# Keys and values of the 64-wide heads by seven block products instead of eight, with the order of the matrix engine written out

## The chip, the cores and the metric

The kernel runs on one core of one Trainium2 chip. A core has a matrix engine (TensorE, PE in the profile), a vector engine (VectorE, DVE), an activation engine (ScalarE, ACT), a general engine (GpSimd, POOL) and a queue engine (SyncE, SP) that mostly issues transfers. Each engine works through its own queue in order and waits on semaphores for the others. Matrix products are written to PSUM, an accumulator memory of eight banks; the other operands lie in SBUF. All data is float32. The metric is the device time of one execution in microseconds (us).

## What is computed

A decoder of two layers on x (8 batches, 256 tokens, 256 features). Layer 0 is self-attention with heads of 16, cross-attention over the context and an expert stage; layer 1 is self-attention, a cross-attention with 16 heads of 64 and an added null key and value, and a stage of 8 experts with a shared expert. The change lies in the cross-attention with heads of 64, cut here to what matters:

```python
x = x + _L1_xattn_ref(_layernorm(x, axis=-1), ctx_2048, Wq, Wkv, null_kv, Wout, ln_scale, ln_bias)
# inside, HEADS, DH = 16, 64; context is (8, 256, 512), Wkv is (512, 2048)
q = _split_heads(jnp.einsum('bnd,df->bnf', x, Wq))
kv = jnp.einsum('bmc,cf->bmf', context, Wkv)
k, v = jnp.split(kv, 2, axis=-1)
k, v = (_split_heads(k), _split_heads(v))
k = jnp.concatenate((nk, k), axis=-2)      # the null key and value
v = jnp.concatenate((nv, v), axis=-2)
sim = jnp.einsum('bhid,bhjd->bhij', q * DH ** -0.5, k)
out = jnp.einsum('bhij,bhjd->bhid', jax.nn.softmax(sim, axis=-1), v)
out = jnp.einsum('bnf,fd->bnd', out.transpose(0, 2, 1, 3).reshape(b, -1, 1024), Wout)
out = (out - mu) * jax.lax.rsqrt(var + EPS) * ln_scale + ln_bias
```

For each batch the keys and values are one product of a 256x512 context with a 512x2048 weight.

## The kernel before

`plain` (line 156) holds the whole decoder; `null_cross_attention` (line 1043) is the stage that is changed. A part that is a loop over the eight batches b follows a first part for b = 0 alone.

**The pieces of one batch.** `keys` (L1058) loads the transposed context `ctxT` and makes kT (features by tokens) by `features` (L1047): four PSUM tiles `fm`, each of two feature blocks of 128, each block four matrix products over the 512 inputs. `vals` (L1065) makes v (tokens by features) in four tiles `vps` of 512 features. `queries` (L1082) makes the null logits `nps` and then qT in four tiles `fm`. `weighted` (L1092) runs the attention: per pair of heads c it forms scores `stx` (L1100), their exponentials `pTx` on ACT (L1104), the sum `both` of the two token halves on POOL (L1106), the column sums `den` on PE (L1114, `sums`) and the weighted values `ox` on PE (L1138). `reciprocals` (L1152) turns `den` into 1/sum on DVE (L1155, L1156) and sends it through DRAM (`rd`, `rs`, L1160 and L1162) to spread it over partitions; `divide` (L1184) multiplies it into oT, half on DVE and half on POOL. `outward` (L1190) is the output projection `wo`, copied to `yx` on ACT, normalised on DVE and POOL (L256 on POOL is the power -1/2 of the variance) and added to x by six POOL instructions (L1203 to L1205). `routed_norm`, `routed_rows` and `routed_scores` (L953 to L966) prepare the previous batch for the expert stage.

**The order.** One batch in the loop is `weighted(b)`, then transposes for batch b+1 and b-1, `reciprocals(b)`, `keys(b+1)`, `routed_scores(b-1)`, `vals(b+1)`, `divide(b)`, `outward(b)`, `queries(b+1)`. Instructions are given to a scheduler that settles each engine's queue when the program is built; where `manual_schedule` names an engine, that engine's order is the order of the text. Here that holds for PE in the last batch and after it. The scheduler also puts in the semaphore waits: an instruction that writes a tile waits for those that read it.

**Product and tiles.** Every 128-wide product goes through one helper as two matmuls of 64 output rows, and each float32 matmul shows as two records in the trace:

```python
def product(out, lhsT, rhs, start, stop):
    for h in (slice(0, 64), slice(64, P)):
        nc.tensor.matmul(out[h], lhsT[:, h], rhs, start=start, stop=stop, skip_group_check=True)
```

All of them carry the helper's line L274, so they are told apart by their tiles. PSUM is shared by three pools (L564 to L566): `mm` with three one-bank tiles (fm, vps, nps, wo, ox and the transposes), `scp` with two tiles of two banks (stx, and hx of the shared expert), `op` with one (den). In SBUF the exponentials take a ring of four buffers with the tag "pT". `load_shared` (L920) loads the shared expert's weights ws13 and ws2 early, before the loop.

Of the kernel before, what the change touches and what calls it, by code (L numbers as in the profile page):

```python
# [28 lines left out]
F32 = mybir.dt.float32  # L29
# [4 lines left out]
ALU = mybir.AluOpType  # L34
# [4 lines left out]
P = 128  # L39
B, S, D = 8, 256, 256  # L40
# [115 lines left out]
def plain(  # L156
# [747 lines left out]
    def ended(t):  # L904

        nc.gpsimd.memset(t[tail:, full, :], 0.0)
        return t
# [9 lines left out]
    norms = [(const.tile([P, 2, 2], F32, name=f"mean{b}"), const.tile([P, 2], F32, name=f"rstd{b}")) for b in range(B)]  # L917
    shared = {}

    def load_shared():  # L920

        router = pool_s.tile([P, 2, E], F32, name="router")
        nc.gpsimd.dma_start(router, a["L1_ffn_router_DE"].rearrange("(c p) e -> p c e", p=P))
        xnT = pool_s.tile([P, 2, B * S], F32, name="xnTe")
        ws13 = w_in(pool_s, a["L1_ffn_ws1_DF"], a["L1_ffn_ws3_DF"], "ws13")
        ws2 = w_out(ended(pool_s.tile([P, NFC, D], F32, name="ws2")), a["L1_ffn_ws2_FD"])
        shared.update(router=router, xnT=xnT, ws13=ws13, ws2=ws2)

    def hidden(mid, first, n, pair, silu):

# [109 lines left out]

    def null_cross_attention(phase):
        work = phase.enter_context(tc.tile_pool(name="d2", bufs=2))
        scale = XD**-0.5

        def features(dst, w, rows, copy):  # L1047
            n = w.shape[1]
            for c2 in range(0, nc8, 2):
                ps = mm.tile([P, 2, S], F32, tag="mm", name="fm")  # L1050
                for i in range(2):
                    for cc in range(n):
                        product(
                            ps[:, i, :], w[:, cc, (c2 + i) * P : (c2 + i + 1) * P], rows[:, cc, :], cc == 0, cc == n - 1
                        )
                copy(dst[:, c2 : c2 + 2, :], ps)

        def keys(b):  # L1058
            ctxT = ctxs.tile([P, CTX // P, S], F32, tag="ctxT", name="ctxT")
            nc.sync.dma_start(ctxT, a["ctx_T"][b].rearrange("(c p) t -> p c t", p=P))  # L1060
            kT = work.tile([P, nc8, S], F32, tag="kT", name="kTx", bufs=1)
            features(kT, wkv_x, ctxT, nc.scalar.copy)
            return ctxT, kT

        def vals(ctxT):  # L1065
            v = work.tile([P, 2, XH, XD], F32, tag="vx", name="vx", bufs=1)
# [13 lines left out]
            return v  # L1080

        def queries(xnT):  # L1082
            nps = mm.tile([P, 2, S], F32, tag="mm", name="nps")
            for k in range(2):
                product(nps[:, 0, :], wn[:, k].rearrange("p g w -> p (g w)"), xnT[:, k, :], k == 0, k == 1)
            qT = work.tile([P, nc8, S], F32, tag="qT", name="qTx", bufs=1)
            features(qT, wq_x, xnT, nc.vector.tensor_copy)
            en = work.tile([P, S], F32, tag="en", name="en")
            nc.scalar.activation(en, nps[:, 0, :], AF.Exp, scale=scale)
            return qT, en  # L1090

        def weighted(kT, v, qT):  # L1092


            def exp_scores(c):
                st = scp.tile([P, 2, 2, S], F32, tag="sc", name="stx")
                for kt in range(2):
                    for g in range(2):
                        rows = slice(XD * g, XD * (g + 1))
                        nc.tensor.matmul(  # L1100
                            st[:, g, kt, :], kT[rows, c, bass.ts(kt, P)], qT[rows, c, :], start=True, stop=True
                        )
                pT = work.tile([P, 2, 2, S], F32, tag="pT", name="pTx", bufs=4)
                nc.scalar.activation(pT, st, AF.Exp, scale=scale)  # L1104
                both = work.tile([P, 2, S], F32, tag="both", name="both", bufs=4)
                nc.gpsimd.tensor_tensor(both, pT[:, :, 0, :], pT[:, :, 1, :], ALU.add)  # L1106
                return pT, both

            oT = work.tile([P, nc8, S], F32, tag="oT", name="oT", bufs=1)
            den = op.tile([P, S], F32, tag="o", name="den")  # L1110

            def sums(c, both):
                for g in range(2):
                    nc.tensor.matmul(  # L1114
                        den[XD * g : XD * (g + 1), :],
                        hot8[:, c, :],
                        both[:, g, :],
                        start=c == 0,
                        stop=c == nc8 - 1,
                        skip_group_check=True,  # L1120
                    )

            def block(c2):
                return [exp_scores(c2 + i) for i in range(2)]


            ahead, before = block(0), []
            for c2 in range(0, nc8, 2):
                now = ahead
                if c2 + 2 < nc8:  # L1130
                    ahead = block(c2 + 2)
                for i, both in enumerate(before):
                    sums(c2 - 2 + i, both)
                o = mm.tile([P, 2, S], F32, tag="mm", name="ox")
                for i, (pT, _) in enumerate(now):
                    for kt in range(2):
                        for g in range(2):
                            nc.tensor.matmul(  # L1138
                                o[XD * g : XD * (g + 1), i, :],
                                v[:, kt, 2 * (c2 + i) + g, :],  # L1140
                                pT[:, g, kt, :],
                                start=kt == 0,
                                stop=kt == 1,
                                skip_group_check=True,
                            )
                (nc.vector.tensor_copy if c2 % 4 else nc.scalar.copy)(oT[:, c2 : c2 + 2, :], o)
                before = [both for _, both in now]
            for i, both in enumerate(before):
                sums(nc8 - 2 + i, both)
            return oT, den  # L1150

        def reciprocals(b, den, en):  # L1152

            r = work.tile([P, S], F32, tag="rx", name="rx")
            nc.vector.tensor_tensor(r, den, en, ALU.add)  # L1155
            nc.vector.reciprocal(r, r)  # L1156
            rd = dram.tile([2, nc8, S], F32, name=f"rd{b}")
# [6 lines left out]
                    rd[g : g + 1].rearrange("g c q -> g (c q)").to_broadcast([XD, nc8 * S]),  # L1164
                )
            nc.gpsimd.tensor_tensor(en, en, r, ALU.mult)
            low = work.tile([P, S], F32, tag="low", name="low")
            nc.vector.tensor_scalar(low, r, 1.0e-25, None, ALU.is_ge)
            nc.vector.scalar_tensor_tensor(
                low, r, 1.0e25, low, ALU.is_le, ALU.mult, accum_out=fit[:, b : b + 1]  # L1170
# [3 lines left out]
        def in_range():  # L1174

            for k in range(3):
                v = dens[:, k].rearrange("p t h -> p (t h)")
                low = work.tile([P, S], F32, tag="low", name="lowk")
                nc.vector.tensor_scalar(low, v, 1.0e-25, None, ALU.is_ge)
                nc.vector.scalar_tensor_tensor(  # L1180
                    low, v, 1.0e25, low, ALU.is_le, ALU.mult, accum_out=fit[:, B + k : B + k + 1]
                )
# [5 lines left out]
                )  # L1188

        def outward(b, oT, en):  # L1190
            y = work.tile([P, 2, D], F32, tag="y", name="yx")
            ps = mm.tile([P, 2, D], F32, tag="mm", name="wo")
            for t in range(2):
                cols = bass.ts(t, P)
# [21 lines left out]


        _, xnT = layernorm_T(0, work, mm)
        ctxT, kT = keys(0)
        v = vals(ctxT)  # L1220
        qT, en = queries(xnT)
        load_shared()
        order = ExitStack()
        for b in range(B):
            more = b + 1 < B
            oT, den = weighted(kT, v, qT)
            if more:
                _, xnT = layernorm_T(b + 1, work, mm)
            else:

                wproj.close()
                late = ctx.enter_context(tc.tile_pool(name="mids", bufs=1, side="right"))

                shared["mid_s"] = [ended(late.tile([P, NFC, 2 * S], F32, name=f"mid{i}")) for i in range(2)]
                routing_tables(late)
                order.enter_context(tc.manual_schedule(engines={mybir.EngineType.PE}))
            if b:
                routed_rows(b - 1, routed_norm(b - 1, work), work)
            rs, old = reciprocals(b, den, en), en
            if b == 1:  # L1240
                in_range()
            if more:
                ctxT, kT = keys(b + 1)
            if more:
                if b:
                    routed_scores(b - 1)
                v = vals(ctxT)
            else:
                for i, _ in enumerate(quarter(0)):
                    if i == 0:  # L1250
                        routed_scores(b - 1)
            divide(oT, rs)
            outward(b, oT, old)
            if more:
                qT, en = queries(xnT)
        order.close()
        with tc.manual_schedule(engines={mybir.EngineType.PE, mybir.EngineType.DVE}):
            for i, _ in enumerate(quarter(1)):
                if i == 1:
# [1227 lines left out]
```

## Time and profile before

Three runs took 1396.82, 1397.8 and 1399.36 us, a median of 1397.8. The execution that was profiled took 1396.5 us, with a span of 1394.8 us between its first and last instruction.

| stretch of the span, us | what runs | length, us | PE busy, us | DVE | ACT | POOL |
|---|---|---|---|---|---|---|
| 0 to 622.00 | layer 0 and self-attention of layer 1 | 622.00 | 596.49 | 309.07 | 274.47 | 184.88 |
| 622.00 to 658.85 | heads of 64: keys, values, queries of b = 0 | 36.85 | 36.75 | 3.89 | 5.67 | 0.86 |
| 658.85 to 721.58 | loop, b = 0 | 62.73 | 62.47 | 11.07 | 15.18 | 19.28 |
| 721.58 to 785.27 | loop, b = 1 | 63.69 | 63.37 | 16.41 | 15.66 | 21.52 |
| 785.27 to 1103.73 | loop, b = 2 to 6 | 318.46 | 316.86 | 71.88 | 78.32 | 104.26 |
| 1103.73 to 1150.85 | loop, b = 7 | 47.12 | 46.80 | 14.15 | 14.37 | 16.92 |
| 1150.85 to 1394.80 | experts | 243.95 | 234.81 | 75.91 | 53.69 | 47.94 |

A batch starts where its first score matmul `stx` starts. PE's clock is granted at 1.00 in every stretch of the loop. Matmuls overlap: a record's duration is its latency, and what a stream of them costs is the distance between starts.

### The profile page before, as it was taken

The page shows a single profiled execution, that of the slowest core. Times are in us where ns is not written, and L with a number is a line of the kernel's source. Part 1 is how long each engine was busy: PE and PEld are TensorE (multiplying, and loading weights), DVE is VectorE, ACT ScalarE, POOL GpSimd, SP SyncE. Part 2 cuts the span into 40 slices and gives each one's busy share as a digit, 9 for nine tenths or more (in the row PEclk, how much of TensorE's full clock was granted, in tenths as well). Part 3 has the DMA queues.
Part 4 walks back from the last instruction along what each step waited for, and adds up shares of the span by engine and source line. Part 5 has one row for each costly group of instructions (what it writes and reads, how often), then busy time and mean ns, then how long its engine had stood idle before and what let it go on. Part 6 is the DMA issues. An engine that isn't in the chain of part 4 may idle for free.

```text
span 1394.8 us, 28640 instructions
## 1 busy us (share of the span) xinstructions
PE 1357.5 (97%) x12198; PEld 884.4 (63%) x12198; DVE 502.4 (36%) x1467; ACT 457.4 (33%) x730; POOL 395.7 (28%) x499
## 2 busy tenths in 40 slices
PE   6999999999999999989999999999999999999998
PEld 3666756756766666665655656565656555688884
DVE  5443563563565654330222213131312225422213
ACT  2555444444444434431222313131322222122221
POOL 4222142052033234220332415152423412400004
PEclk9999999999999999999999999999999999999999
DMA  8960000000000006010101010110101010779954
GB/s 312 345 205 16 9 24 9 8 24 1 1 9 2 2 9 221 1 53 26 32 16 31 16 47 2 46 32 16 32 1 32 1 31 5 283 289 414 402 209 127
DMA packets 46921, 116.56 MB, mean 84 GB/s; under 512 B 8273, under 2 KB 30401, under 8 KB 42433
## 3 DMA queue, kind: packets, MB, share of 16 engines
q1 hardware_dynamic: 38912, 92.74, 19.3%
q0 software_dynamic: 5152, 18.89, 3.6%
q10 hardware_dynamic: 2720, 3.02, 0.6%
q8 instruction: 98, 1.61, 0.5%
q14 instruction: 39, 0.31, 0.1%
HBM read 104.00 MB, written 27.93 MB: 95 GB/s over the span
## 4 chain that ended last, share of the span: by engine, by line
PE 85%; DVE 5%; POOL 4%; issue 1%; ACT 1%; DMA 0%; ACTq 0%; POOLq 0%; DVEq 0%; SPq 0%
PE fm L274 12%; PE st L332 9%; PE o L364 9%; PE vps L274 8%; PE h L274 6%; PE wo L274 4%; PE ox L1138 4%; PE stx L1100 4%; PE out L1475 3%; PE out L1292 3%; PE h L947 3%; PE qk L274 3%; PE hx L947 3%; PE tr L281 3%; PE den L1114 2%; PE ao L274 2%
## 5 line engine op out<-in xcount | busy, mean ns | idle before, releaser
L364 PE MATMUL o<-pT,padv 128*64 128x256 f32 (+1 forms) x1536 | 171.6, 365 | 1.1 <-POOL pT L344 1.1
L341 ACT ACTIVATE pT<-st 128x1024 f32<-128x1024 f32 (+1 forms) x128 | 110.5, 915 | 88.8 <-PE st L332 87.9
L364 PEld LDWEIGHTS o<-pT,padv 128*64 128x64 f32 x1536 | 103.1, 137 | 52.7 <-issue 10.0
L332 PE MATMUL st<-qm,kT 64*128 64x256 f32 (+1 forms) x1024 | 117.2, 367 | 0.9 <-DVE qm L310 0.6
L274 PE MATMUL fm<-ctxT,wkv_x 128*64 128x256 f32 x1024 | 112.9, 380 | 0.0
L274 PE MATMUL vps<-wkv_x,ctxT 128*64 128x512 f32 x512 | 111.8, 593 | 0.0
L332 PEld LDWEIGHTS st<-qm,kT 64*128 64x128 f32 x1024 | 90.1, 189 | 26.0 <-issue 15.6
L274 PEld LDWEIGHTS fm<-ctxT,wkv_x 128*64 128x64 f32 x1024 | 73.0, 137 | 37.3 <-issue 1.3
L1106 POOL TENSOR_TENSOR both<-pTx 128x512 f32<-128x512 f32 x64 | 79.6, 1273 | 57.4 <-ACT pTx L1104 33.8
L1104 ACT ACTIVATE pTx<-stx 128x1024 f32<-128x1024 f32 x64 | 62.1, 1021 | 89.9 <-PE stx L1100 86.8
L274 PE MATMUL h<-xrT,w 128*64 128x128 f32 (+1 forms) x1936 | 86.9, 250 | 1.4 <-issue 1.4
L274 PEld LDWEIGHTS h<-xrT,w 128*64 128x64 f32 x1936 | 84.3, 137 | 4.4 <-issue 2.1
L274 PEld LDWEIGHTS vps<-wkv_x,ctxT 128*64 128x64 f32 x512 | 36.4, 137 | 68.9 <-issue 68.6
L341 ACT ACTIVATE pT<-st,kbias 128x1024 f32<-128x1024 f32 x64 | 68.0, 1113 | 28.7 <-PE st L332 28.7
L256 POOL TENSOR_TENSOR lnrs<-lnve,mhalf 128x2 f32<-128x2 f32 x48 | 34.2, 717 | 147.0 <-DVE lnve L254 95.2
L332 PE MATMUL st<-qm,memk 64*128 64x256 f32 x512 | 68.8, 393 | 0.5
L939 ACT ACTIVATE sl<-h 128x128 f32<-128x128 f32 (+1 forms) x114 | 35.4, 310 | 96.1 <-PE h L274 56.7
L1100 PE MATMUL stx<-qTx,kTx 64*128 64x256 f32 x512 | 64.3, 391 | 2.5 <-ACT pTx L1104 2.5
L940 DVE TENSOR_TENSOR midr<-sl,h 128x128 f32<-128x128 f32 x102 | 29.4, 288 | 100.5 <-PE h L274 68.6
L251 DVE BATCH_NORM_STATS2 lxst<-yx 128x6 f32<-128x256 f32 x16 | 6.0, 418 | 162.7 <-ACT yx L1198 162.7
L274 PE MATMUL qk<-l_wqkv,xnT 128*64 128x512 f32 x256 | 62.6, 610 | 0.7 <-ACT xnT L284 0.7
L344 POOL TENSOR_SCALAR_AFFINE_SELECT pT<-pT 128x512 f32<-128x512 f32 x64 | 39.5, 638 | 83.1 <-ACT pT L341 79.8
(274 smaller groups left out, 2080.7 us busy)
## 6 DMA issues: line engine op xcount, KB each, us to landing
w<-packs SPq DMA_DIRECT2D x22, 1408.0 KB
w<-packs SPq DMA_DIRECT2D x22, 768.0 KB
rs<-rd SPq DMA_DIRECT2D x16, 512.0 KB
packs<-L_ffn_w_eDF SPq DMA_DIRECT2D x8, 704.0 KB
packs<-L_ffn_w_eDF SPq DMA_DIRECT2D x8, 640.0 KB
packs<-L_ffn_w_eFD SPq DMA_DIRECT2D x8, 640.0 KB
ctxT<-ctx_T SPq DMA_DIRECT2D x8, 512.0 KB
wkv_x<-L_xattn_Wkv POOLq DMA_DIRECT2D x1, 4096.0 KB, 17.3
```

Of the source, the lines that this page charges most:

```text
L274: nc.tensor.matmul(out[h], lhsT[:, h], rhs, start=start, stop=stop, skip_group_check=True)
L281: nc.tensor.transpose(ps[:, c, t * P : (t + 1) * P], rows[:, t, c * P : (c + 1) * P], ident)
L332: nc.tensor.matmul(st[:, g, i, :n], kT[rows, c, bass.ts(kt, P)], qm[rows, 2 * mq + i, c, q0:], start=True, stop=True,)
L341: nc.scalar.activation(pT[:, :, :, :n], st[:, :, :, :n], AF.Exp, scale=scale, **kb)
L364: nc.tensor.matmul(o[64 * i : 64 * i + 64, mq, q0:], v_pad[:, kt, 4 * c + 2 * mq + i, 2 * g : 2 * g + 2, :], pTs[kt][:, g, i, : S - q0], s ...
L947: nc.tensor.matmul(h, shared["ws13"][:, c, lo : lo + P], shared["xnT"][:, c, bass.ts(q, 2 * S)], start=c == 0, stop=c == 1)
L1100: nc.tensor.matmul(st[:, g, kt, :], kT[rows, c, bass.ts(kt, P)], qT[rows, c, :], start=True, stop=True)
L1104: nc.scalar.activation(pT, st, AF.Exp, scale=scale)
L1106: nc.gpsimd.tensor_tensor(both, pT[:, :, 0, :], pT[:, :, 1, :], ALU.add)
L1138: nc.tensor.matmul(o[XD * g : XD * (g + 1), i, :], v[:, kt, 2 * (c2 + i) + g, :], pT[:, g, kt, :], start=kt == 0, stop=kt == 1, skip_group ...
L1292: nc.tensor.matmul(ps, mid[:, i, lo : lo + P], w2[:, i, :], start=i == 0, stop=i == NFC - 1)
L1475: nc.tensor.matmul(ps[h], mid[:, i, h], sets[k % len(sets)][1][:, i, :], start=i == 0, stop=i == NFC - 1, skip_group_check=True,)
```

## The change

In the loop, keys and values of batches 1 to 7 are no longer made by `keys` and `vals` but by `seven`: context and weight are each cut into two by two blocks, and each of keys (m = 0) and values (m = 1) is made from seven block products in Strassen's manner (with the shared sums of Winograd's form). Batch 0 keeps the old way.

- `sums_of_weights` makes the weight sums t1, t2, t4 and (in place) t3 once, 16 DVE subtractions of 128x512, around the products of batch 0; `sums_of_context` makes s1 to s4 for each batch, four DVE instructions of 128x256.
- A product for keys is 16 matmuls with 128 moving columns in place of 256; one for values is 4 matmuls with 512.
- The running sums stay in PSUM: `xy` is one `scp` tile of two banks, xb and yb; products 1, 6, 7, 4 go into xb and 5, 3 into yb, and product 2 into an `mm` tile zb. Between products ACT copies p1, p5 and u out of it (into the "pT" ring) and DVE adds them to later products to form three of the four result blocks; ACT copies the fourth.
- PE's order is written out in every batch from the first product on: k1, the last sums `den` of weighted (moved behind k1 as `rest`), k2, k5, k6, v1, k7, k3, k4, v2, v5, v6, `routed_scores`, nps, v7, v3, v4, the queries' four fm, and then wo. The queries thus move from behind `outward` to ahead of it.
- The context of batch b+1 is loaded at the top of batch b. The buffers of y, low and rx go from two to one.
- The shared expert's weights ws13, ws2 and the mid tiles are allocated in the last batch, where the weights of keys and queries lay; their loads follow those weights' last use.

```diff
-    def load_shared():
-
+    def load_router():
         router = pool_s.tile([P, 2, E], F32, name="router")
         nc.gpsimd.dma_start(router, a["L1_ffn_router_DE"].rearrange("(c p) e -> p c e", p=P))
-        xnT = pool_s.tile([P, 2, B * S], F32, name="xnTe")
-        ws13 = w_in(pool_s, a["L1_ffn_ws1_DF"], a["L1_ffn_ws3_DF"], "ws13")
-        ws2 = w_out(ended(pool_s.tile([P, NFC, D], F32, name="ws2")), a["L1_ffn_ws2_FD"])
-        shared.update(router=router, xnT=xnT, ws13=ws13, ws2=ws2)
+        shared.update(router=router, xnT=pool_s.tile([P, 2, B * S], F32, name="xnTe"))
+
+    def load_shared(pool):
+
+        shared["ws13"] = w_in(pool, a["L1_ffn_ws1_DF"], a["L1_ffn_ws3_DF"], "ws13")
+
+        shared["mid_s"] = [ended(pool.tile([P, NFC, 2 * S], F32, name=f"mid{i}")) for i in range(2)]
+        shared["ws2"] = ended(pool.tile([P, NFC, D], F32, name="ws2"))
...
+        wsum = wproj.enter_context(tc.tile_pool(name="wsum", bufs=1, side="right"))
...
+        half = CTX // P // 2
+        def w_block(j, k):
+            return wkv_x.rearrange("p c (m k f) -> p c m k f", m=2, k=2)[:, half * j : half * (j + 1), :, k, :]
+        tw = wsum.tile([P, 3, half, 2, XH * XD // 2], F32, name="tw")
+        t1, t2, t3, t4 = tw[:, 0], tw[:, 1], w_block(0, 1), tw[:, 2]
+        def sums_of_weights(n):
+            dst, p, q = (
+                (t1, w_block(0, 1), w_block(0, 0)),
+                (t2, w_block(1, 1), t1),
+                (t4, w_block(1, 0), t2),
+                (t3, w_block(1, 1), w_block(0, 1)),
+            )[n]
+            for m in range(2):
+                for c in range(half):
+                    nc.vector.tensor_tensor(dst[:, c, m], p[:, c, m], q[:, c, m], ALU.subtract)
+        def sums_of_context(ctxT):
+            def block(i, j):
+                return ctxT[:, half * j : half * (j + 1), bass.ts(i, P)]
+            sw = wsum.tile([P, 3, half, P], F32, tag="sw", name="sw")
+            s1, s2, s3, s4 = sw[:, 0], sw[:, 1], block(1, 0), sw[:, 2]
+            nc.vector.tensor_tensor(s1, block(1, 0), block(1, 1), ALU.add)
+            nc.vector.tensor_tensor(s2, s1, block(0, 0), ALU.subtract)
+            nc.vector.tensor_tensor(s4, block(0, 1), s2, ALU.subtract)
+            nc.vector.tensor_tensor(s3, block(0, 0), block(1, 0), ALU.subtract)
+            return block(0, 0), block(0, 1), s4, block(1, 1), s1, s2, s3
+        w_terms = w_block(0, 0), w_block(1, 0), w_block(1, 1), t4, t1, t2, t3
+        def seven(terms, m, dst):
+            xy = scp.tile([P, 2, 2 * S], F32, tag="sc", name=f"kv{m}")
+            xb, yb = xy[:, 0], xy[:, 1]
+            def product_of(n, bank, fresh):
+                s, t = terms[n - 1], w_terms[n - 1][:, :, m, :]
+                for i in range(4 if m == 0 else 1):
+                    for c in range(half):
+                        if m == 0:
+                            args = bank[:, bass.ts(i, P)], t[:, c, bass.ts(i, P)], s[:, c, :]
+                        else:
+                            args = bank, s[:, c, :], t[:, c, :]
+                        product(*args, fresh and i == 0 and c == 0, c == half - 1)
...
+            def kept(bank, name):
+                t = work.tile([P, 2 * S], F32, tag="pT", name=f"kv{name}{m}", bufs=4)
+                nc.scalar.copy(t, bank)
+                return seen(t)
+            product_of(1, xb, True)
+            p1 = kept(xb, "p")
+            yield
+            zb = mm.tile([P, 2 * S], F32, tag="mm", name=f"kvz{m}")
+            product_of(2, zb, True)
+            nc.vector.tensor_tensor(of(0, 0), p1, seen(zb), ALU.add)
+            product_of(5, yb, True)
+            p5 = kept(yb, "v")
+            yield
+            product_of(6, xb, False)
+            u = kept(xb, "u")
+            yield
+            product_of(7, xb, False)
+            nc.vector.tensor_tensor(of(1, 1), p5, seen(xb), ALU.add)
+            yield
+            product_of(3, yb, False)
+            nc.vector.tensor_tensor(of(0, 1), u, seen(yb), ALU.add)
+            product_of(4, xb, False)
+            nc.scalar.copy(of(1, 0), seen(xb))
+            yield
...
         for b in range(B):
             more = b + 1 < B
-            oT, den = weighted(kT, v, qT)
+            if more:
+                ctxT = context(b + 1)
+            oT, den, rest = weighted(kT, v, qT)
             if more:
                 _, xnT = layernorm_T(b + 1, work, mm)
+                terms = sums_of_context(ctxT)
             else:
+                rest()
                 wproj.close()
...
+                load_shared(late)
...
+            if more:
+                order.enter_context(tc.manual_schedule(engines={mybir.EngineType.PE}))
+                kT = work.tile([P, nc8, S], F32, tag="kT", name="kTx", bufs=1)
+                v = work.tile([P, 2, XH, XD], F32, tag="vx", name="vx", bufs=1)
+                k7, v7, q = seven(terms, 0, kT), seven(terms, 1, v), queries(xnT)
+                next(k7)
+                rest()
             rs, old = reciprocals(b, den, en), en
...
             if more:
-                ctxT, kT = keys(b + 1)
-            if more:
+                for made in (k7, k7, v7, k7, k7, v7, v7):
+                    next(made)
                 if b:
                     routed_scores(b - 1)
-                v = vals(ctxT)
+                next(q)
+                next(v7)
+                next(v7)
+                next(q)
+                qT, en = next(q)
...
             divide(oT, rs)
             outward(b, oT, old)
-            if more:
-                qT, en = queries(xnT)
-        order.close()
+            order.close()
```

## The prediction

> **What bounds the kernel now.** I read the page first (busy times, then the chain), then the instructions in order of time through batch 0 of the loop, then the rows of the other products by shape.
>
> ```profile
> PE 1357.5 (97%) x12198; PEld 884.4 (63%) x12198; DVE 502.4 (36%) x1467; ACT 457.4 (33%) x730; POOL 395.7 (28%) x499
> PE 85%; DVE 5%; POOL 4%; issue 1%; ACT 1%; DMA 0%; ACTq 0%; POOLq 0%; DVEq 0%; SPq 0%
> ```
>
> PE is the bound, and in the loop it has no slack to give: batch 0 has 62.47 us busy in 62.73. So every matmul taken out counts, and so does every wait put in. Batch 0 in order of time (start, length, engine):
>
> ```profile
> 660.03 1.95 ACT L1104 ACTIVATE pTx<-stx 128x1024 f32<-128x1024 f32 x2 [7.60 <-PE stx L1100]
> 661.14 4.95 POOL L1106 TENSOR_TENSOR both<-pTx 128x512 f32<-128x512 f32 x4 [33.34 <-ACT pTx L1104]
> 666.89 1.08 PE L1114 MATMUL den<-both,hot 128*64 128x256 f32 x8
> ...
> 676.79 1.03 PE L1114 MATMUL den<-both,hot 128*64 128x256 f32 x8
> 678.34 14.03 PE L274 MATMUL fm<-ctxT,wkv_x 128*64 128x256 f32 x128
> 678.40 1.75 DVE L1156 RECIPROCAL rx<-rx 128x256 f32<-128x256 f32 x1
> 680.30 0.64 SPq L1160 DMA_DIRECT2D rd<-rx  x2
> 688.71 2.38 DVE L1186 TENSOR_TENSOR oT<-oT,rs 128x512 f32<-128x512 f32 x2 [7.35 <-DMA rs<-rd]
> 692.21 13.90 PE L274 MATMUL vps<-wkv_x,ctxT 128*64 128x512 f32 x64
> 705.94 0.60 PE L274 MATMUL wo<-nvw,en 128*64 128x256 f32 x4
> 713.93 0.59 ACT L1198 COPY yx<-wo 128x512 f32<-128x512 f32 x1 [7.18 <-PE wo L274]
> 715.80 0.72 POOL L256 TENSOR_TENSOR lxrs<-lxve,mhalf 128x2 f32<-128x2 f32 x1 [23.58 <-DVE lxve L254]
> 720.83 0.73 POOL L1205 TENSOR_TENSOR x<-x,yx 128x256 f32<-128x256 f32 x1
> ```
>
> Keys take 678.34 to 692.21, 13.87 us; values to 705.94, 13.73 us. Their four PSUM tiles rotate, so no copy is waited for. Ahead of `den`, POOL's `both` are done early. Behind `wo` runs a chain ACT, DVE, POOL of 7.6 us (713.93 to 721.56), beside the queries' matmuls. Three rows price what the change adds: a product with 128 moving columns, a wait of PE for an ACT copy of 128x512, and a DVE addition of 128x512 that reads PSUM.
>
> ```profile
> 1247.07 5.02 PE L274 MATMUL h<-xrT,w 128*64 128x128 f32 x88
> 618.62 0.59 ACT L284 COPY xnT<-tr 128x512 f32<-128x512 f32 x1 [2.16 <-PE tr L281]
> 619.26 1.95 PE L274 MATMUL ao<-l_wo,xnT 128*64 128x256 f32 x16 [0.68 <-ACT xnT L284]
> 1128.79 0.69 DVE L940 TENSOR_TENSOR mid<-slx,hx 128x512 f32<-128x512 f32 x1 [1.22 <-ACT slx L939]
> ```
>
> **The matmuls saved.** Keys: 7 products of 16 matmuls, two records each, are 224 records with 128 columns. In the `h` row 88 such records take 5.02 us, the last of them 0.27: 4.75 / 87 = 54.6 ns apart, so 12.23 us. Values: 7 x 4 x 2 = 56 records at 13.73 / 64 = 214.5 ns, 12.01 us. Together 24.24 in place of 27.60: 3.36 us a batch, 23.5 us in seven batches. From below: the key row's weight loads fill 73.0 us for 1024 records, 71.3 ns each; if loads set the pace at 128 columns, keys take 16.0 us and 0.4 us a batch is lost. I take the `h` row, the same shape.
>
> [...]
>
> **Six waits of PE in each batch.** The built program gives each instruction with the semaphores that it waits for. xb and yb are halves of one PSUM tile, and the waits are set for the whole tile: product 6 (into xb) waits for the copy of p5 out of yb; product 3 (yb) for the addition that reads product 7 out of xb; product 4 (xb) for the addition that reads product 3 out of yb. In each pair the waited-for read begins only when the product just ahead on PE has ended. Keys and values have these three each; all later PE work is queued behind them. The wait of product 7 for u is covered (v1 lasts 1.72 us for keys; `sc` and nps, 0.6 + 0.87, for values), and product 5's for p1 by product 2 and more.
>
> Price: `ao` shows 0.68 us of idle PE around a 0.59 us copy. A stream also loses its overlap: a record of 128 columns lasts 0.27 us while the next pair would start 0.11 after its pair, 0.16. An ACT wait is then 0.84, say 0.85; with 0.69 in place of 0.59 a DVE wait is 0.95. Bounds: the bare idle, 0.68 and 0.78, and 0.2 more each for a DVE or ACT that is busy.
>
> One is longer, that of k4. DVE's queue holds the two divisions (L1186) ahead of k3's addition, and they wait for `rs`. From k1's start at 0: k1 ends 1.74, den 2.60, k2 4.35, k5 6.09, wait, k6 6.94 to 8.69, v1 10.40, k7 12.15, wait, k3 13.10 to 14.84. In the trace the last `den` ends at 677.82, the reciprocal at 680.15 and the divisions start at 688.71: 2.33 and 8.56 later. Here den's last record ends at 2.77, so divisions run 13.66 to 16.04, the addition to 16.73, and k4 starts at 16.8: 1.95 instead of 0.95. It could be 0.95 if `rs` came 1 us sooner, 3.0 if it came 1 us later.
>
> Sum: 0.85 + 0.95 + 1.95 for keys, 0.85 + 0.95 + 0.95 for values: 6.5 us a batch, 45.5 us in seven.
>
> [...]
>
> **The queries' place.** They covered the chain behind `wo`. Now the next batch's scores follow `wo` directly, and POOL's queue has five of the six L1203 to L1205 instructions ahead of `both` 0, the sixth ahead of `both` 1, and L958 and two L256 ahead of `both` 2. Count from the first score matmul. The chain starts at 0.1 (yx); in the trace the fifth instruction ends 6.8 later, so `both` 0 runs 6.9 to 8.1, the sixth to 8.8, `both` 1 to 10.05. `den` of pair 0 comes at 8.04 in the trace (666.89 - 658.85) and is hardly late; that of pair 1, due at 8.5, starts at 10.1: 1.6 us. Then (L256 twice is 1.51) `both` 2 to 7 end at 13.0, 14.2, 15.5, 16.7, 17.95, 19.2 against `den` at 14.3, 14.8, 17.0, 17.4 and after 19.5: no wait. This happens in batches 1 to 7: 11.2 us. Bounds: 0, if POOL catches up; 2.6, with POOL a further microsecond behind. Removing the queries' own place saves nothing, their matmuls are the same.
>
> **What costs nothing, and its cover.** The weight sums (16 DVE instructions) lie beside batch 0's products, where DVE is busy 3.89 of 36.85 us; t3 is queued ahead of the queries' copies and ends about when the first is due, 2.6 us after the values; uncovered it would cost 2 us once. The context sums (four of about 0.4) stand behind the last addition on DVE and ahead of the query copies, which are due 3.4 us later. ctxT is asked for a batch ahead. The shared weights: SP issues them when the last queries of b = 6 are done, 7.9 us ahead of the scores of b = 7; the POOL copy behind them came 6.2 us after the first issue in the trace (621.3, 627.5), and the chain needs POOL 2 us after the scores start: 3.7 us to spare; a miss delays batch 7 alone. `rest` comes after k1, when `both` 7 is long done. The single y, rx and low buffers were last read half a batch before.
>
> **Sum.** -23.5 + 45.5 + 11.2 = +33.2 us on the profiled execution's 1396.5 (span 1394.8, 1.7 around it): 1429.7. The median of the runs lies 1.3 above that execution; I say 1430.
>
> **Rivals.** (a) The change does what its arithmetic says: the waits are passed before PE reaches them and POOL catches up. 1396.5 - 23.5 = 1373. For it: PE is the bound and the products rotate. Against: each read starts at the end of the very product ahead. (b) Only POOL's lateness stays: 1396.5 - 23.5 + 11.2 = 1384; this needs the six waits to cost under 0.3 us each. (c) Only the six waits stay, POOL keeping up because `both` takes its place in time: 1396.5 - 23.5 + 45.5 = 1418.5. (d) The halved key products run at the pace of the weight loads: 26 us more than the sum, 1456. The sign turns where waits and POOL cost under 3.36 us a batch; I have 8.1.
>
> **How the numbers follow.** My forecast (both waits at their prices) 0.68; (c) 0.12; (d) 0.11; (b) 0.06; (a) 0.03. Lowest for the forecast: 4 waits at 0.78 and 2 at 0.68, POOL 0.9: 2.0 us a batch, 1411. Highest that I believe: 0.2 more on each wait, `rs` 1 us later, POOL 1 us later: 8.1 + 1.2 + 1.0 + 1.0 - 3.36 = 7.9 a batch, 1452, with all of it at once unlikely, so 1448. The range 1410 to 1448 holds the forecast and (c) and leaves out (a), (b) and (d). Differences within 0.2% are what a measurement of this kernel can't tell from none; faster 0.09, same 0.01, slower 0.90.
>
> **What would show it.** In the profile after: the loop's batches near 68.5 us in place of 63.7; in PE's waits, rows of about 14 for kv behind ACT (0.7 us each) and 28 behind DVE (0.8, seven of them 1.8), and 7 for `den` behind POOL (1.6); key records 55 ns apart; no wait of `hx` for ws13. Wrong if kv rows show no waits (then b or a), if `both` 1 is done 8.5 us after the scores begin (c), or if PE is busy without gaps and still longer (d).

## The result and the profile after

The change makes the kernel slower: four runs took 1437.25 to 1443.21 us, a median of 1440.26, against 1397.31 for four runs of the kernel before. The ratio is 1.031, with a 95% interval of 1.028 to 1.033. The forecast was 1430, in a range of 1410 to 1448. The profiled execution took 1443.21 us (span 1441.5), 46.7 more than the one of before (1396.5); the terms below are weighed against that.

The page of the changed kernel, busy times and chain:

```profile
PE 1353.3 (94%) x12814; PEld 905.8 (63%) x12814; DVE 557.2 (39%) x1553; ACT 457.6 (32%) x730; POOL 393.2 (27%) x499
PE 73%; DVE 9%; POOL 7%; DMA 4%; issue 2%; ACT 1%; SPq 0%; DVEq 0%; POOLq 0%; ACTq 0%
```

PE's share falls from 97% to 94% of a longer span, and the chain that was PE's for 85% now runs through DVE, POOL and transfers for a fifth of the time (9% before). PE waits, and its waits say for whom. In the list of PE's waits (tile and line that waits, engine, tile and line waited for; us in total, times, longest; `kv` is the tile xy of the running sums, `kvp`, `kvv` and `kvu` are ACT's copies of p1, p5 and u, `kvz` is the tile zb, and `kTx` and `vx` are the keys and values):

```profile
PE kv L274 <- DVE kTx L1172: 13.9, 7, 2.6
PE kv L274 <- ACT kvv L1153: 10.4, 14, 0.7
PE den L1231 <- POOL both L1223: 8.8, 7, 1.3
...
PE kv L274 <- DVE vx L1169: 6.0, 7, 0.9
PE kv L274 <- DVE kTx L1169: 6.0, 7, 0.9
PE kv L274 <- DVE vx L1172: 5.5, 7, 0.8
```

These are the rows that were forecast: 14 waits behind ACT's copies, 28 behind DVE's additions, 7 of `den` behind POOL. None of them is in the profile before, where the list of PE's waits between 658.85 and 1150.85 us has one row alone:

```profile
PE stx L1100 <- ACT pTx L1104: 2.5, 8, 0.3
```

One batch of the loop in order of time (start, length, engine, line; in brackets the idle time ahead and who ended it):

```profile
804.00 1.27 POOL L1223 TENSOR_TENSOR both<-pTx 128x512 f32<-128x512 f32 x1
805.23 0.73 POOL L1325 TENSOR_TENSOR x<-x,yx 128x256 f32<-128x256 f32 x1
805.92 1.26 POOL L1223 TENSOR_TENSOR both<-pTx 128x512 f32<-128x512 f32 x1
807.23 0.65 PE L1231 MATMUL den<-both,hot 128*64 128x256 f32 x4 [1.25 <-POOL both L1223]
...
824.25 0.58 ACT L1153 COPY kvv<-kv 128x512 f32<-128x512 f32 x1 [3.77 <-PE kv L274]
824.89 1.97 PE L274 MATMUL kv<-sw,tw 128*64 128x128 f32 x32 [0.74 <-ACT kvv L1153]
...
830.44 0.69 DVE L1169 TENSOR_TENSOR kTx<-kvv,kv 128x512 f32<-128x512 f32 x1 [6.09 <-PE kv L274]
831.18 1.97 PE L274 MATMUL kv<-sw,wkv_x 128*64 128x128 f32 x32 [0.86 <-DVE kTx L1169]
832.20 2.36 DVE L1306 TENSOR_TENSOR oT<-oT,rs 128x512 f32<-128x512 f32 x2 [1.07 <-DMA rs<-rd]
834.48 0.67 DVE L1172 TENSOR_TENSOR kTx<-kvu,kv 128x512 f32<-128x512 f32 x1
835.21 2.45 PE L274 MATMUL kv<-ctxT,tw 128*64 128x128 f32 x32 [2.06 <-DVE kTx L1172]
837.44 3.14 PE L274 MATMUL kvz<-wkv_x,ctxT 128*64 128x512 f32 x8
```

Read each pair downward: a product ends, a copy or addition of 0.6 to 0.7 us reads its bank, and the next product, into the other bank of the tile, begins when that read is over. Ahead of k4 (835.21) the two divisions stand between k3 and its addition. POOL's last addition to x (805.23) pushes the second `both` back, and `den` waits 1.25 us.

The last two rows hold what was not foreseen. k4's 32 records last 2.45 us in place of 1.92 to 1.97, and v2's 8 records 3.14 in place of 1.89, though nothing is waited for. Busy time in two stretches around the wait of k4, of this batch (two rows) and of a batch without such slow rows (two rows); columns: stretch, length, then busy time (and instructions) of PE, PEld, DVE, ACT, POOL, the granted clock of PE, the share of the DMA engines and GB/s:

```profile
833.12:836.54 3.42, 1.36 (x26) 1.33 (x26) 2.04 (x2) 0.00 (x0) 2.56 (x2) 1.00 0.00 0
836.54:839.95 3.41, 3.41 (x18) 1.62 (x16) 0.00 (x0) 0.58 (x1) 0.00 (x0) 0.50 0.02 5
901.39:904.80 3.41, 1.97 (x32) 1.73 (x32) 3.01 (x4) 0.00 (x0) 2.28 (x2) 1.00 0.02 5
904.80:908.22 3.42, 2.72 (x38) 2.15 (x40) 0.65 (x2) 0.58 (x1) 1.18 (x1) 1.00 0.00 0
```

For 3.41 us PE's clock was granted at one half. It happens in the four batches whose k4 waits 2.06 us or more (2.06, 2.46, 2.48, 2.63), and not in the three with 1.33 to 1.52. Below, such a stretch is called a spell of half clock. Those four batches are 71.0 to 71.6 us long; of the others, b = 3 and 4 take 68.6 and 68.8 and b = 0 (no wait for POOL) 66.2. Before, a batch took 63.69, batch 0 62.73.

### The profile page after: what moved, and what is told of

The parts are those of the page before. It is cut to its first block, busy times and chain, and to the rows that moved or that the text cites. A ratio compares the mean times of both kernels' runs of the same rounds, so it can differ in the third digit from the quotient of the medians.

```text
span 1441.5 us, 30007 instructions
## 1 busy us (share of the span) xinstructions
PE 1353.3 (94%) x12814; PEld 905.8 (63%) x12814; DVE 557.2 (39%) x1553; ACT 457.6 (32%) x730; POOL 393.2 (27%) x499
## 4 chain that ended last, share of the span: by engine, by line
PE 73%; DVE 9%; POOL 7%; DMA 4%; issue 2%; ACT 1%; SPq 0%; DVEq 0%; POOLq 0%; ACTq 0%
PE st L332 9%; PE o L364 9%; PE kv L274 7%; PE h L274 6%; PE fm L274 5%; PE wo L274 4%; DMA rs<-rd 3%; PE out L1614 3%; PE ox L1255 3%; PE out L1431 3%; PE h L950 3%; PE tr L281 2%; PE qk L274 2%; PE hx L950 2%; PE ao L274 2%; PE den L1231 2%
## 5 line engine op out<-in xcount | busy, mean ns | idle before, releaser
L332 PEld LDWEIGHTS st<-qm,kT 64*128 64x128 f32 x1024 | 90.0, 189 | 26.0 <-issue 15.6
L332 PE MATMUL st<-qm,memk 64*128 64x256 f32 x512 | 68.8, 393 | 0.5
L256 POOL TENSOR_TENSOR lxrs<-lxve,mhalf 128x2 f32<-128x2 f32 x8 | 5.6, 704 | 219.0 <-DVE lxve L254 219.0
L1255 PE MATMUL ox<-pTx,vx 128*64 128x256 f32 x512 | 61.1, 381 | 0.0
L1217 PEld LDWEIGHTS stx<-qTx,kTx 64*128 64x128 f32 x512 | 46.1, 186 | 20.3 <-issue 9.2
L274 PE MATMUL wo<-wout_x,oT 128*64 128x256 f32 x512 | 58.0, 379 | 0.0
L332 PEld LDWEIGHTS st<-qm,memk 64*128 64x128 f32 x512 | 48.0, 186 | 15.1 <-issue 5.1
```

Of the source, the lines that this page charges most:

```text
L332: nc.tensor.matmul(st[:, g, i, :n], kT[rows, c, bass.ts(kt, P)], qm[rows, 2 * mq + i, c, q0:], start=True, stop=True,)
L1217: nc.tensor.matmul(st[:, g, kt, :], kT[rows, c, bass.ts(kt, P)], qT[rows, c, :], start=True, stop=True)
L1255: nc.tensor.matmul(o[XD * g : XD * (g + 1), i, :], v[:, kt, 2 * (c2 + i) + g, :], pT[:, g, kt, :], start=kt == 0, stop=kt == 1, skip_group ...
```

## The experiments

The theory from this trace: (1) the waits come from one tile that covers two banks; (2) the queries' place costs by itself, through POOL; (3) the divisions ahead of k3's addition make k4's wait long; (4) the half clock follows from PE's idle time in fixed windows of 3.41 us, the length of the stretch above. The rivals stand in the expectations: the waits only move, the products are slow by themselves, POOL is late for another reason. Times below are medians; ratios are to runs of the kernel before on the same chip.

**Separate banks.** The two running sums get tiles of their own; the order on PE stays.

```diff
-            xy = scp.tile([P, 2, 2 * S], F32, tag="sc", name=f"kv{m}")
-            xb, yb = xy[:, 0], xy[:, 1]
+            if m == 0:
+                zb, xb, yb = [mm.tile([P, 2 * S], F32, tag="mm", name=f"kv{n}{m}") for n in "zxy"]
+            else:
+                xb, yb = [scp.tile([P, 2, 2 * S], F32, tag="sc", name=f"kv{n}{m}")[:, 0] for n in "xy"]
+                zb = mm.tile([P, 2 * S], F32, tag="mm", name=f"kvz{m}")
...
-            zb = mm.tile([P, 2 * S], F32, tag="mm", name=f"kvz{m}")
```

> The sums of each product set (xb and yb) get a PSUM tile and bank of their own; order of the matmuls unchanged. Theory (six waits because one tile covers both banks): the rows of PE waiting in kv for kvv, kTx and vx go, 41.8 us, with about 0.16 us of lost overlap at each of the 42 places (6.7), and with them the four spells of half clock that follow the longest waits (some 1.7 each, 6.7); the wait of den for POOL stays (8.8). Of the changed kernel's 1443 that leaves about 1388, just under the kernel before (ratio 0.99). Rival 1 (the waits only move, to product 4 behind the divisions or to the next reader): 1405 to 1430 with new rows of kv behind DVE. Rival 2 (the seven products are slow by themselves, the waits being only where it shows): no lower than 1425.

Measured: 1384.53 us, ratio 0.991 (0.990 to 0.993). All rows of kv are gone from PE's waits; `den` behind POOL stays with 8.8 us. Part of one batch in order of time, k5 (806.60), k6, k3 and k4 with the reads of the product ahead of each:

```profile
806.60 1.92 PE L274 MATMUL kvy<-sw,tw 128*64 128x128 f32 x32
...
808.35 1.92 PE L274 MATMUL kvx<-sw,tw 128*64 128x128 f32 x32
808.62 0.58 ACT L1156 COPY kvv<-kvy 128x512 f32<-128x512 f32 x1 [3.77 <-PE kvy L274]
...
813.56 1.92 PE L274 MATMUL kvy<-sw,wkv_x 128*64 128x128 f32 x32
813.84 0.69 DVE L1171 TENSOR_TENSOR kTx<-kvv,kvx 128x512 f32<-128x512 f32 x1 [5.13 <-PE kvx L274]
815.30 1.92 PE L274 MATMUL kvx<-ctxT,tw 128*64 128x128 f32 x32
815.52 0.69 DVE L1174 TENSOR_TENSOR kTx<-kvu,kvy 128x512 f32<-128x512 f32 x1 [0.99 <-PE kvy L274]
```

The reads are the same, but each now lies beside a product into the other bank: ACT copies kvy while k6 writes kvx, DVE reads kvx while k3 writes kvy. The products follow one another at 1.745 us (806.60, 808.35; 813.56, 815.30), 54.5 ns for each of 32 records. Batches 1 to 6 are 61.95 us long and none has a half clock. So the waits were the loss, and the products themselves run as their rows of before said. Rivals 1 and 2 fall.

**The queries back behind wo.** In the changed kernel, with the shared tile.

```diff
                 next(v7)
                 next(v7)
-                next(q)
-                qT, en = next(q)
...
             outward(b, oT, old)
+            if more:
+                next(q)
+                qT, en = next(q)
```

> The four query products go back behind the outward product, as in the kernel before; everything else is as in the changed kernel. Theory (POOL's chain behind wo collides with the next batch's scores): the seven waits of den for both (8.8 us) go, with some 0.1 of overlap each: 1443 less 9.5, about 1433; the six waits in kv stay as they are. Rival (POOL is late for another reason, such as its speed beside the shorter batch): den still waits, 1443.

Measured: 1424.89 us, ratio 1.021 (1.019 to 1.022), lower than expected; the 1443 that the expectation starts from is the longest of the four runs of the changed kernel. The row of `den` is gone, and the waits of kv are still there:

```profile
PE kv L274 <- DVE kTx L1172: 12.8, 7, 2.4
PE kv L274 <- ACT kvv L1153: 10.4, 14, 0.7
...
PE kv L274 <- DVE kTx L1169: 6.0, 7, 0.9
```

The rest of the gain is the half clock: in this execution no batch has one, although four of its waits for k4 are 1.84 to 2.4 us long. One of them in order of time, and busy time in the two windows (the grid is the one on which this execution's half clock in layer 0 begins) that share the wait between them:

```profile
1030.03 1.97 PE L274 MATMUL kv<-ctxT,tw 128*64 128x128 f32 x32 [2.37 <-DVE kTx L1172]
```

```profile
1025.72:1029.13 3.41, 1.93 (x32) 1.69 (x32) 2.12 (x2) 0.00 (x0) 2.08 (x2) 1.00 0.00 0
1029.13:1032.54 3.41, 2.51 (x36) 2.09 (x38) 0.84 (x2) 0.50 (x1) 1.37 (x1) 1.00 0.02 5
```

2.37 us of idle time and a full clock: the length of the wait alone doesn't decide. The three others (1.84, 2.21 and 2.30) lie across a border of the same grid too, and no window of this loop has less than 1.74 us of busy PE.

**Both together.** Separate banks, and the queries behind wo.

> Separate banks and the queries back behind wo together. Theory: both terms go and the arithmetic of the seven products is left, 23.5 us under the kernel before plus the small rest: 1374 to 1380, ratio 0.983 to 0.988. Rival (the gains overlap, or a new wait takes their place): 1385 or more, ratio 0.99 and above.

Measured: 1373.91 us, ratio 0.985 (0.983 to 0.986): faster than the kernel before by 1.5%, and what the matmul arithmetic of the forecast gives. Its batches 1 to 6 take 60.39 us, 3.30 less than before. Against the run with separate banks alone a batch is 1.56 us shorter: the price of the queries' place.

**The queries' place alone.** The kernel before, with `queries(xnT)` moved ahead of `divide` and `outward`; keys and values by eight as they were.

```diff
+            if more:
+                qT, en = queries(xnT)
             divide(oT, rs)
             outward(b, oT, old)
-            if more:
-                qT, en = queries(xnT)
```

> The kernel before with one part of the change alone: the queries are asked for ahead of the outward product instead of behind it; keys and values stay as they were. Theory (the place of the queries costs by itself, through POOL's chain): den waits for both in batches 1 to 7, 1.56 us a batch as between the two runs with separate banks, so 10.9 us more than before, ratio 1.008. Rival (the collision needs the shorter batch of the seven products): no change, ratio 1.000.

Measured: 1412.6 us, ratio 1.009 (1.008 to 1.011). Batches 1 to 6 take 65.25 us, 1.56 more than before, and PE's list of waits has the same row:

```profile
PE den L1114 <- POOL both L1106: 8.8, 7, 1.3
```

The term needs neither seven products nor their waits. The run is 13.3 us longer than the kernel before on the same chip (1399.30); in the profiled execution what goes beyond the 10.9 of seven batches lies behind the loop, and it was not followed.

**All divisions on POOL.** In the changed kernel.

```diff
-                (nc.vector if c2 % 4 else nc.gpsimd).tensor_tensor(
+                nc.gpsimd.tensor_tensor(
```

> All four divisions of a batch go to POOL, none to DVE, so that the addition of k3 has no transfer of rs ahead of it on DVE. Theory: product 4 of the keys waits 0.86 in every batch in place of 1.33 to 2.63 (7.9 us less), and since no window of time holds so much idle PE any more, the half-clock spells in the loop go too (6.7): about 1429. Rival (the slow k4 and v2 come from the products or their banks, not from the idle time ahead): 1435, with spells still there.

Measured: 1427.19 us, ratio 1.022 (1.021 to 1.024). k4 now waits like the others, and the loop has no half clock; batches 1 to 6 take 68.06 us each, so the rival falls:

```profile
PE kv L274 <- DVE vx L1172: 5.5, 7, 0.8
PE kv L274 <- DVE kTx L1172: 5.5, 7, 0.8
```

**k4's wait, lengthened by set amounts.** On top of the run above, the keys' addition behind k3 is done two or three times.

```diff
-            nc.vector.tensor_tensor(of(0, 1), u, seen(yb), ALU.add)
+            for _ in range(3 if m == 0 else 1):
+                nc.vector.tensor_tensor(of(0, 1), u, seen(yb), ALU.add)
```

> As the run with all divisions on POOL, and the keys' addition behind k3 is done twice (the second writes the same values), so product 4 of the keys waits one addition longer in every batch, 1.55 in place of 0.86. Both theories on the clock expect 0.69 x 7 = 4.8 more than that run, 1432, and no half clock in the loop: in no window of 3.41 us are there 1.71 us of idle PE.

> The same with the addition done three times: product 4 waits 2.24 in each of the seven batches. Grid theory (the clock is decided at the end of fixed windows of 3.41 us, and halved for the next one when PE was busy for less than half of it, 1.71): only batches whose wait lies with 1.71 or more inside one window see the half clock, about two thirds of them, each for 3.41 us at a price of 1.67: 1427 + 9.7 + 7 to 8 = 1444. Rival (any wait above some 2 us trips it): all seven, 1449. Rival (no clock effect): 1437.

Measured, one execution each: 1435.6 and 1450.24 us, on another chip than the run with all divisions on POOL; there the kernel before took 1399.30 us, 2.8 more than the 1396.49 on that run's chip. With two additions k4 waits 1.5 us, a batch takes 68.79 and the loop has no half clock. With three it waits 2.24 in every batch, and five of the seven batches have the half clock. Six of the seven k4 in order of time (the seventh has the half clock too):

```profile
695.44 3.07 PE L274 MATMUL kv<-ctxT,tw 128*64 128x128 f32 x32 [2.24 <-DVE kTx L1173]
766.27 1.97 PE L274 MATMUL kv<-ctxT,tw 128*64 128x128 f32 x32 [2.23 <-DVE kTx L1173]
835.77 3.44 PE L274 MATMUL kv<-ctxT,tw 128*64 128x128 f32 x32 [2.23 <-DVE kTx L1173]
906.95 2.96 PE L274 MATMUL kv<-ctxT,tw 128*64 128x128 f32 x32 [2.24 <-DVE kTx L1173]
978.12 2.48 PE L274 MATMUL kv<-ctxT,tw 128*64 128x128 f32 x32 [2.23 <-DVE kTx L1173]
1049.32 1.97 PE L274 MATMUL kv<-ctxT,tw 128*64 128x128 f32 x32 [2.24 <-DVE kTx L1173]
```

The same wait, with two outcomes. All five spells, and two in layer 0, begin on one grid of 3.413 us. Batches 1 and 5, which escape (69.5 us in place of 71.2, so a spell costs 1.67), have their wait across a border of the grid. The windows of the second row:

```profile
760.98:764.39 3.41, 2.19 (x38) 1.73 (x32) 0.99 (x2) 0.00 (x0) 0.84 (x1) 1.00 0.31 60
764.39:767.81 3.42, 1.54 (x28) 1.54 (x30) 1.75 (x3) 0.00 (x0) 3.42 (x4) 1.00 0.02 5
767.81:771.22 3.41, 3.41 (x24) 1.26 (x20) 0.69 (x1) 0.58 (x1) 0.69 (x1) 1.00 0.00 0
```

This also corrects the theory: that the bound is half of the window, 1.71 us, was the author's estimate between the 1.36 and 1.97 us of the rows further up; here 1.54 us busy is under it, and the clock stayed at 1.00. The loop from batch 0 to 6 is 18.5 us longer than with single additions: 10.1 of waits (15.6 less 5.5) and five times 1.67. The other 4 us to 1450 lie outside the loop and were not followed; the other chip may account for most of them.

**Other cover for the reads.** One tile for both banks again, but keys and values alternate on PE so that a product stands between each read and the product that waits for it. The generator of `seven` also pauses between products 3 and 4; the queries are behind wo.

```diff
-                for made in (k7, k7, v7, k7, k7, v7, v7):
+                for made in (k7, v7, k7, v7, k7, v7, k7, v7, k7, v7):
                     next(made)
                 if b:
                     routed_scores(b - 1)
                 next(q)
                 next(v7)
-                next(v7)
...
             product_of(3, yb, False)
             nc.vector.tensor_tensor(of(0, 1), u, seen(yb), ALU.add)
+            yield
             product_of(4, xb, False)
```

> One PSUM tile for both banks as in the changed kernel, so the six waits on the whole tile are still set, but the products of keys and values alternate on TensorE (k1, den, k2, k5, v1, k6, v2, v5, k7, v6, k3, v7, k4, scores, v3, nps, v4), so that another product or more lies between a read and the product that waits for it; queries behind wo. Theory (what costs is that each read starts when the product just ahead ends): the waits vanish without any new bank, and the time comes to 1374 to 1384; what may stay is up to 1 us a batch at k3, since the divisions stand ahead of k7's addition on DVE. Rival (the two-bank tile costs something beyond the waits, or alternating weights costs overlap): above 1395.

Measured: 1381.46 us, ratio 0.987 (0.986 to 0.989). One row of kv is left in PE's waits, the one at k3, in five batches:

```profile
PE kv L274 <- DVE kTx L1169: 3.0, 5, 1.0
```

So five of the six waits go by order alone, with the tile as it was. Batches 0 to 6 take 426.2 us, 4.3 more than with separate banks and the queries behind wo (421.9): 3.0 for the waits that are left and, at 0.22 of lost overlap each (worked out below), 1.1. The two-bank tile costs next to nothing beyond its waits.

## Why the prediction was right in sign and low by 10 to 14 us

The working by its steps, with the profiled execution (46.7 us more than before) as the measure. Batch lengths are from one score start to the next, b = 0 to 6.

| step | forecast, us | measured, us | from |
|---|---|---|---|
| The matmuls saved | -23.5 | -23.0 | banks and queries against before: 59.52 - 62.73, then 60.39 - 63.69 six times |
| Six waits of PE in each batch | +45.5 | +51.1 | changed kernel less separate banks, 57.8 in seven batches, less the half clock |
| The queries' place | +11.2 | +10.9 | 1.56 in each of seven batches, with separate banks and in the kernel before |
| (half clock after k4's wait) | 0 | +6.7 | 4 x 1.67 |
| outside the loop | 0 | +1.0 | the rest |
| sum | +33.2 | +46.7 | |

**The matmuls saved: right.** The `h` row's 54.6 ns for 128 columns was the price: 54.5. The weight loads, 71.3 ns each by the estimate from the key row of before, did not set the pace, so rival (d) is out.

**Six waits: the places right, the price a little low.** The idle times were 0.74 behind ACT, 0.79 to 0.86 behind DVE. The lost overlap is larger than the 0.16 that was put in: b = 3 is 68.61 us against 61.95 with separate banks, 6.66 for 5.32 of idle time, so 0.22 at each wait. k4's was to be 1.75 idle and 0.2; the idle time came to 1.99 on average, since from the reciprocal's end to the divisions it took 8.54 to 9.84 us (9.19 on average). The forecast took 8.56 from one batch of the trace of before, whose batches 0 to 6 have 8.34 to 9.02 (8.52 on average). What scatters this transfer through DRAM was not settled. Per batch 7.3 in place of 6.5. In the run with separate banks ACT and DVE read one bank while PE wrote another (ACT's copy of kvy at 808.62, k6 into kvx from 808.35), and the 41.8 us in the rows of kv were gone. In the changed kernel it was the waits, set for the whole tile, that kept them apart.

**The queries' place: right**, 1.56 against 1.6 a batch, with POOL's queue as told: the second `both` ended at 807.18, 10.04 us after the first score matmul (10.05 in the forecast), so the rest that rival (c) hoped for wasn't there.

**What failed: the step "Six waits of PE in each batch", at k4, charged a gap at its length and no more.** The matmuls behind it were put at their usual rate. In four batches they ran 3.41 us at half clock, at 1.67 each: b = 1 takes 71.44 us against 68.61 of b = 3, 2.83 more, of which 1.15 is k4's longer wait (2.48 against 1.33). The trace of before had such a spell to read. Two windows of the kernel before, around a transpose in layer 0 that waits 2.54 us for DVE:

```profile
198.11:201.53 3.42, 0.88 (x7) 0.55 (x6) 1.60 (x4) 1.53 (x2) 2.29 (x3) 1.00 0.27 79
201.53:204.94 3.41, 3.41 (x29) 1.77 (x31) 1.50 (x2) 1.43 (x3) 0.00 (x0) 0.50 0.00 0
```

The clock row of the page, in 40 slices of 35 us, hides a spell of 3.4 us. That the time still fell into the stated range is in part luck: the range's upper side was kept for longer waits, a later `rs` and a later POOL, and a lower clock, half of the miss of 13.5 us, was not among them. The covers under "What costs nothing" held: ws13 caused no wait of `hx`, and the weight and context sums appear in no row of PE's waits.

Rival (a), the bare arithmetic of 1373, was not this kernel, but it is the kernel with separate banks and the queries behind wo, 1373.91.

## What to carry to other kernels

In a program built as this one, a semaphore wait follows the tile, not the bank (41.8 us of waits with one tile for both sums, none with two): where two running sums in PSUM are read and written in turn, each should have a tile of its own, or a product of another sum should stand between the read and the write. When an instruction group is moved on the busiest engine, look at what it had been covering in the queues of the others (here 1.56 us a batch). And a gap of about 2 us on PE can cost nearly double (here 2.06 and 1.67 more), so it is worth removing from a queue such as DVE's whatever waits for a transfer ahead of work that PE needs.

## What the runs showed of the hardware that was not expected

The half clock comes on a grid. In the changed kernel six spells of 3.41 us (two in layer 0, four in the loop) begin at 201.66, 307.48, 764.86, 836.54, 1044.76 and 1116.43 us, multiples of 3.413 us from one another; so they do in the run with three additions. In the loop a spell begins at the end of a window in which PE had little to do, 0.3 to 1.3 us after PE has taken up work again, and lasts one window. There, windows with 0.85 to 1.36 us of busy PE led to it and one with 1.54 did not; at the start of the kernel before, one with 1.67 us did, made of 7 records. Busy time in the trace is thus not quite what counts, and the exact bound stays open. A wait of 2.06 us was enough in the changed kernel, and one of 2.37 us across a border was harmless in the run with the queries behind wo. The four runs of the changed kernel fit this: from 1443.21 to 1437.25 us their mean granted clock goes from 0.990 to 0.994; 0.004 of 1440 us are about 5.8 us, and the times differ by 5.96.
